# Another order for the beginning of a convolution and attention kernel: biases by products, one norm moved to the keys, last stores on ScalarE's queue

## The chip, the cores and the metric

The kernel runs on one core of a Trainium2 chip. A core has TensorE (PE: matrix products into PSUM), VectorE (DVE), ScalarE (ACT), GpSimd (POOL) and SyncE (SP); each works through its own queue of instructions in order, and they wait for each other by semaphores. DMA transfers are issued from the queues of SP, ACT and POOL. The metric is the device time of one execution in microseconds (us), the median of several runs.

## The reference

For a batch x of shape (4, 384, 48, 48), all in float32:

```
inv   = bn_gamma * rsqrt(bn_var + 1e-5)
local = depthwise_conv7x7(x, conv_w) * inv + (bn_beta - bn_mean * inv)
xn    = layernorm(x over channels) * ln_gamma + ln_beta
q, k, v = split(xn @ qkv_w.T + qkv_b)         # 8 heads of 48
q     = q + layernorm(local over channels)    # same ln_gamma, ln_beta
a     = softmax(q @ k.T * 48**-0.5) @ v       # over all 2304 positions
out   = x + a @ proj_w.T + proj_b
```

## The kernel before

**Tiles.** Channels lie on partitions, in CC = 3 blocks of 128. An image of 2304 positions is cut into NG = 6 groups of G = 384 (eight rows of 48). With four images there are NT = 24 groups, numbered t = 6b + g. All weights stay on the chip.

**Stages.** The beginning loads weights, folds the norm's gain into the projection weights, and makes keys, values and queries of image 0 for all six groups (`from_x`, steps of two products each, taken by `next(making)`). Attention of one group runs over 12 slots with two halves each (`attend`): four pairs of heads, three slots for each. `score` makes products of keys and queries (line 730), ScalarE takes their exponential (L738), and `weigh` multiplies by the values (L751). Between two images lies the stage of keys: for each of its six groups values, keys and queries of the new image and the output products of the old one. Behind the last attention (line 978 on) the output products of the last image's six groups remain: the tail.

**Convolution.** Its 49 taps for three channel blocks are 147 VectorE instructions for each group (L245 for the first tap, L249 for the others), which run behind TensorE's work all through the kernel. For the first group ten taps of channel block 0 are done on TensorE with diagonal matrices (`first_products`, L268). A generator (`conv_ops`) yields after each instruction; `convolve_first(n)` takes n in the beginning, `convolve(point)` takes as many as `plan` has given to a point of the schedule. `plan` starts from what the beginning has done, adds estimates of VectorE's spare time at each point (`spare`, `spare_at_keys`), and sets a rate so that group t's convolution is complete before slot 6 of group t - 1 (slot 8 for t = 1), where its layernorm begins.

**Norms.** Two kinds of layernorm go along: of the convolution's result (one for each group), and of x for the coming image (`norm_x` in the slots, `norms_x` at the keys). Each sums over channels twice. In the beginning and for t = 0 the sums are products with a constant matrix (L376, L381); later they go over DRAM (`out`, L418 and L419, two trips for each norm). VectorE adds, centres (L391, L436) and scales (L460, L610); ScalarE squares (L354, L359) and takes the root. `query_end` (L619) adds the normed convolution to the queries. X_LATER = 3: three of an image's x-norms lie in the attention slots of the image before (its groups 3 to 5), three at the image's own keys.

**Biases.** The layernorm's offset beta reaches keys, values and queries as a bias. `shift_rows` multiplies beta by the weights, which gives one row of 384 numbers; `rows_out` copies it out of PSUM (L561), stores it to DRAM on ScalarE's queue (L566) and loads it back as a column on POOL's (L104); `key_bias` and `query_bias` add it. ScalarE folds the gain into the weights in `scale_values` and `scale_rows`.

**Order.** The order on TensorE, VectorE and ScalarE is that of the program's text. The queue of SP is ordered by the compiler of the kernel, by its own estimates of when things are ready. SP issues nearly all loads and stores. A tile taken again from a pool waits until its former use is over: residuals (`xr`) and fetched attention results (`af`) have two buffers each. `finish` (L706) adds bias and residual, and issues the store of the result (L709). PSUM is handed out in two alternating pools (`two_banks`).

**Flag.** At the end the kernel counts reciprocals of softmax denominators that are out of a safe range (`judge`: L1018 to L1024), loads the count into registers of all engines (L1027) and jumps past a second, careful version if it is zero.

The last group's attention result is multiplied with its reciprocals within the tail:

```
        if last:
            ao = outputs[before][0]
            nc.vector.tensor_mul(ao, ao, rb)
        else:
            load_residual(before + 1)
```

Of the kernel before, what the change touches and what calls it, by code (L numbers as in the profile page):

```python
# [28 lines left out]
LAG = 2  # L29
PE_TAPS = 10  # L30
# [14 lines left out]
def unshifted_pass(  # L45
# [101 lines left out]
    nc.gpsimd.memset(eps, LN_EPS)  # L147
    nc.sync.dma_start(out=norms[:, 0:4], in_=bn)
# [78 lines left out]
    def conv_ops(t):  # L227
# [9 lines left out]
        for i, tap in enumerate(taps):  # L237
            for c in range(CC) if t or i >= PE_TAPS else range(1, CC):
                part = window(slab, acc[:, c, :], g, first, end, c, tap)
                if not part:  # L240
                    continue
                src, dst = part
                weight = cw[:, c, tap : tap + 1]
                if tap == taps[0]:
                    nc.vector.tensor_scalar(  # L245
                        dst, src, weight, shift[:, c : c + 1], ALU.mult, ALU.add
                    )
                else:
                    nc.vector.scalar_tensor_tensor(dst, src, weight, dst, ALU.mult, ALU.add)  # L249
                yield  # L250
# [28 lines left out]
    def spare(t, s, half):  # L279
# [3 lines left out]
        if b + 1 < B and g >= X_LATER:  # L283
            time -= {(3, 1): 2.3, (4, 1): 2.2, (5, 1): 2.3, (7, 0): 0.4, (8, 0): 2.6}.get(
                (s, half), 0.0
            )
# [10 lines left out]
    def spare_at_keys(g, h):  # L297
        time = 4.6 - {0: 0.6, 4: 1.2}.get(h, 0.0)
        if g < NG - X_LATER:
            time -= {0: 2.3, 2: 2.2, 4: 2.3}.get(h, 0.0)  # L300
        if 0 < g <= NG - X_LATER:
            time -= {1: 0.4, 3: 2.6}.get(h, 0.0)
# [3 lines left out]
    for t in range(NT):  # L306
        if t % NG == 0 and t:
            points += [("kv", t, g, h) for g in range(NG) for h in range(5)]
            room += [spare_at_keys(g, h) for g in range(NG) for h in range(5)]
# [233 lines left out]
    rows = [None] * CC  # L543

    def shift_rows(some):
        r = two_banks()
        for j, i in enumerate(some):
            rows[i] = r[0:1, j, :C]
            project(
                rows[i],  # L550
                lambda c: beta[:, c : c + 1],
                lambda c: staged[i][:, c, :] if i < 2 else w_v[:, c, :],
            )

    def rows_out(some):

        row = work.tile([P, C, CC], F32, tag="rb", name="row", bufs=1)
        row = row.rearrange("p c n -> p (c n)")[0:1, 0 : C * len(some)]
        row = row.rearrange("o (c n) -> o c n", n=len(some))
        for j, i in enumerate(some):  # L560
            nc.scalar.copy(row[:, :, j], rows[i])  # L561
        bias = dram.tile([C, len(some)], F32, tag=f"bias{some[0]}", name="bias", bufs=1)
        columns = const.tile(
# [971 lines left out]
```

## Time and profile before

| what | us |
|---|---|
| median of 3 runs (2885.15 to 2888.23) | 2886.48 |
| the profiled execution | 2889.06 |
| its span, first to last instruction | 2887.3 |
| TensorE busy | 2841.7 |
| VectorE busy | 2351.0 |
| ScalarE busy | 1649.4 |
| first attention product, image 0 | 146.4 |
| last attention product ends | 2828.7 |
| last VectorE instruction ends | 2881.3 |

An instruction's line reads: start, length, engine, line of the program, operation, output<-inputs, partitions and sizes, how many were merged; in brackets the engine's idle time before it and what ended that. A line of waits reads: who waited for whom, total us, times, longest. In a line of stretches each engine's busy time is followed by its number of instructions, and the last columns are the granted clock of TensorE (1.00 is full speed), the share of the DMA engines' time, and GB/s.

### The profile page before, as it was taken

The page shows a single profiled execution, that of the slowest core. Times are in us where ns is not written, and L with a number is a line of the kernel's source. Part 1 is how long each engine was busy: PE and PEld are TensorE (multiplying, and loading weights), DVE is VectorE, ACT ScalarE, POOL GpSimd, SP SyncE. Part 2 cuts the span into 40 slices and gives each one's busy share as a digit, 9 for nine tenths or more (in the row PEclk, how much of TensorE's full clock was granted, in tenths as well). Part 3 has the DMA queues.
Part 4 walks back from the last instruction along what each step waited for, and adds up shares of the span by engine and source line. Part 5 has one row for each costly group of instructions (what it writes and reads, how often), then busy time and mean ns, then how long its engine had stood idle before and what let it go on. Part 6 is the DMA issues. An engine that isn't in the chain of part 4 may idle for free.

```text
span 2887.3 us, 70195 instructions
## 1 busy us (share of the span) xinstructions
PE 2841.7 (98%) x29474; PEld 1398.5 (48%) x29474; DVE 2351.0 (81%) x4661; ACT 1649.4 (57%) x2340; POOL 21.6 (1%) x89
## 2 busy tenths in 40 slices
PE   8999999999999999999999999999999999999997
PEld 4544444444554444444455445555555544444443
DVE  7899999999888988878888888888788787787301
ACT  4366666666326666666623666666642466666661
POOL 2000000000000000000000000000000000000000
PEclk9999999999999999999999999999999999999999
DMA  6101121112221111111132112102113110100003
GB/s 114 40 4 37 43 49 35 23 38 44 71 79 33 39 35 41 31 38 24 37 94 68 27 30 51 34 23 45 38 42 89 45 30 21 41 23 15 14 20 119
DMA packets 103948, 124.37 MB, mean 43 GB/s; under 512 B 43603, under 2 KB 89284, under 8 KB 103621
## 3 DMA queue, kind: packets, MB, share of 16 engines
q1 hardware_dynamic: 102160, 119.61, 17.4%
q8 instruction: 233, 3.82, 0.6%
q14 instruction: 95, 0.77, 0.1%
q0 software_dynamic: 960, 0.07, 0.0%
q10 hardware_dynamic: 500, 0.11, 0.0%
HBM read 81.98 MB, written 27.04 MB: 38 GB/s over the span
## 4 chain that ended last, share of the span: by engine, by line
PE 89%; DVE 8%; DMA 2%; ACT 0%; issue 0%; POOL 0%; SPq 0%; ACTq 0%; DVEq 0%; POOLq 0%
PE r L730 35%; PE o L751 35%; PE r L465 9%; PE o L465 9%; DVE acc L249 6%; DVE xr L706 0%; DMA xr<-in_x_dram 0%; DMA staged<-in_qkv_wT_dram 0%; DMA columns<-bias 0%; DVE sq L365 0%; DMA taps_in<-in_conv_w_dram 0%; PE r L376 0%; DMA xn<-in_x_dram 0%; DMA w_v<-in_qkv_wT_dram 0%; DVE sq L364 0%
## 5 line engine op out<-in xcount | busy, mean ns | idle before, releaser
L738 ACT ACTIVATE pt<-r 128x768 f32<-128x768 f32 x1728 | 1400.6, 811 | 757.7 <-PE r L730 741.7
L249 DVE SCALAR_TENSOR_TENSOR acc<-slab,vec,acc 128x368 f32<-128x368 f32 (+5 forms) x3447 | 1753.9, 586 | 0.0
L751 PE MATMUL o<-pt,v 64*64 64x384 f32 x13824 | 1428.2, 482 | 0.0
L730 PE MATMUL r<-xn,k 48*64 48x384 f32 x10368 | 1073.7, 483 | 10.2 <-ACT pt L738 8.2
L751 PEld LDWEIGHTS o<-pt,v 64*64 64x64 f32 x13824 | 528.0, 132 | 592.9 <-issue 588.3
L730 PEld LDWEIGHTS r<-xn,k 48*64 48x64 f32 x10368 | 395.7, 133 | 457.9 <-issue 409.2
L730 PE MATMUL r<-qt,kt 48*64 48x384 f32 x3456 | 356.3, 482 | 0.1
L730 PEld LDWEIGHTS r<-qt,kt 48*64 48x64 f32 x3456 | 130.7, 132 | 149.2 <-issue 138.7
L649 DVE TENSOR_TENSOR ao<-o,ao 113x384 f32<-113x384 f32 x72 | 40.0, 556 | 198.8 <-PE r L730 181.6
L465 PE MATMUL o<-xn,w_qk 128*128 128x384 f32 x450 | 153.3, 486 | 0.0
L465 PE MATMUL r<-xn,w_qk 128*128 128x384 f32 x414 | 141.0, 486 | 0.0
L465 PEld LDWEIGHTS o<-xn,w_qk 128*128 128x128 f32 x450 | 85.5, 190 | 59.6
L465 PEld LDWEIGHTS r<-xn,w_qk 128*128 128x128 f32 x414 | 78.7, 190 | 54.9
L497 ACT COPY v<-o 128x384 f32<-128x384 f32 x46 | 20.0, 482 | 135.2 <-PE o L465 135.2
L465 PE MATMUL o<-w_v,xn 128*128 128x384 f32 x276 | 93.4, 487 | 0.0
L465 PE MATMUL r<-af,w_o 128*128 128x384 f32 x228 | 81.8, 508 | 5.2 <-DMA af<-held 3.1
L649 DVE TENSOR_TENSOR aot<-o,aot 113x384 f32<-113x384 f32 x24 | 13.4, 557 | 79.2 <-ACT aot L640 62.2
L364 DVE TENSOR_TENSOR sq<-sq 128x384 f32<-128x384 f32 x47 | 26.1, 555 | 55.6 <-ACT sq L359 55.5
L465 PEld LDWEIGHTS o<-w_v,xn 128*128 128x128 f32 x276 | 52.2, 190 | 37.5 <-issue 1.8
L465 PEld LDWEIGHTS r<-af,w_o 128*128 128x128 f32 x228 | 44.5, 197 | 38.5 <-DVE xr L706 4.5
L706 DVE SCALAR_TENSOR_TENSOR xr<-o,pb,xr 128x384 f32<-128x384 f32 x26 | 16.1, 618 | 53.4 <-ACT xn L516 42.4
L503 ACT ACTIVATE k<-o,qkb 128x384 f32<-128x384 f32 x48 | 25.5, 579 | 53.0 <-PE o L465 53.0
(125 smaller groups left out, 1058.7 us busy)
## 6 DMA issues: line engine op xcount, KB each, us to landing
xr<-in_x_dram SPq DMA_DIRECT2D x24, 576.0 KB
out_dram<-xr SPq DMA_DIRECT2D x72, 192.0 KB
slab<-in_x_dram SPq DMA_DIRECT2D x32, 378.0 KB
held<-ao SPq DMA_DIRECT2D x20, 576.0 KB
af<-held SPq DMA_DIRECT2D x20, 576.0 KB
xn<-in_x_dram SPq DMA_DIRECT2D x48, 216.0 KB
rb<-rden SPq DMA_DIRECT2D x48, 216.0 KB
slab<-in_x_dram SPq DMA_DIRECT2D x16, 297.0 KB
```

The costliest lines, as they stand in the source:

```text
L249: nc.vector.scalar_tensor_tensor(dst, src, weight, dst, ALU.mult, ALU.add)
L364: nc.vector.tensor_add(self.buf[:, 0, :], src[:, 0, :], src[:, 1, :])
L465: nc.tensor.matmul(dst, lhsT=weights(c), rhs=src(c), start=c == 0, stop=c == CC - 1)
L497: nc.scalar.copy(v[:, blk, :, 0:HD], r[:, :C].rearrange("p (h d) -> p h d", d=HD))
L503: nc.scalar.activation(k[:, u, :], r[:, :G], AF.Identity, bias=qkb[:, 1, u : u + 1])
L649: nc.vector.tensor_add(dst, sums[0 : 64 + HA, 1, :G], dst)
L706: nc.vector.scalar_tensor_tensor(xr[:, co, :], m, pb[:, co : co + 1], xr[:, co, :], ALU.add, ALU.add)
L730: nc.tensor.matmul(r[h, j, :G], lhsT=kk[:, blk * P + h.start : blk * P + h.stop], rhs=qq, start=True, stop=True,)
L738: nc.scalar.activation(pt, r[:, :, :G], AF.Exp, scale=SCALE)
L751: nc.tensor.matmul(sums[halves[j], i, :G], lhsT=values[t // NG, kb // NB][h, first : first + 64], rhs=pt[h, j, :], start=kb == 0, stop=kb ...
```

## The change

- **Beginning.** All six groups of image 0 now follow one order. The first group's special order of convolution steps (8 of channel block 0's taps first, then blocks 1 and 2, then the rest) is new, and so are the numbers of steps taken at each place.
- **Biases.** `rows_out` goes. `shift_rows` now writes rows to partition 0 or 64 and copies them to SBUF, in the weights' head order; `columns` turns each row into columns by products of one row with the number one. The queries' row is made within the first group.
- **Norms.** For image 1 alone, `later` is 4: four of its x-norms lie beside its keys and two in the attention slots of image 0. The estimates for `plan` follow.
- **Tail.** The stores of the last six groups are issued on ScalarE's queue. The second group's residual and attention result are requested in the last attention, later ones one group earlier in the text. The count comes ahead of the second group's products, the last multiply after the third group, and the register loads ahead of the last group's products.

```diff
+AHEAD = 8
...
+    one = const.tile([P, 1], F32, tag="one", name="one")
+    nc.gpsimd.memset(one, 1.0)
...
-        for i, tap in enumerate(taps):
-            for c in range(CC) if t or i >= PE_TAPS else range(1, CC):
...
+        order = [(tap, c) for tap in taps for c in range(CC)]
+        if t == 0:
+            mine = [(tap, 0) for tap in taps[PE_TAPS:]]
+            order = mine[:AHEAD] + [o for o in order if o[1]] + mine[AHEAD:]
+        for tap, c in order:
...
-        if b + 1 < B and g >= X_LATER:
+        if b + 1 < B and g >= later(b + 1):
...
+    def later(b):
+
+        return X_LATER + (b == 1)
+
-    def spare_at_keys(g, h):
+    def spare_at_keys(b, g, h):
         time = 4.6 - {0: 0.6, 4: 1.2}.get(h, 0.0)
-        if g < NG - X_LATER:
+        if g < later(b):
             time -= {0: 2.3, 2: 2.2, 4: 2.3}.get(h, 0.0)
-        if 0 < g <= NG - X_LATER:
+        if 0 < g <= later(b):
             time -= {1: 0.4, 3: 2.6}.get(h, 0.0)
...
-    rows = [None] * CC
+
+    row = work.tile([P, CC, P], F32, tag="rb", name="row", bufs=1)
+
+    def of_row(i):
+        return slice(0, 1) if i == 2 else slice(64, 65)
 
     def shift_rows(some):
         r = two_banks()
+        for c in range(CC):
+            for i in some:
+                nc.tensor.matmul(
+                    r[of_row(i), i % 2, :C],
+                    lhsT=beta[:, c : c + 1],
+                    rhs=staged[i][:, c, :] if i < 2 else w_v[:, c, :],
+                    start=c == 0,
+                    stop=c == CC - 1,
+                )
+        for i in some:
+            src, dst = r[of_row(i), i % 2, :C], row[of_row(i)]
+            dst = dst.rearrange("o u (h d) -> o u h d", h=2)
+            nc.scalar.copy(
+                dst[:, :, :, 0:HD], src[:, 0:288].rearrange("o (u h d) -> o u h d", h=2, d=HD)
+            )
+            nc.scalar.copy(
+                dst[:, :, :, HD:64],
+                src[:, 288:384].rearrange("o (h u r) -> o u h r", h=2, r=16),
+            )
+
+    def columns(some):
+
+        m = two_banks()[:, :, 0:CC]
         for j, i in enumerate(some):
...
+            for c in range(CC):
+                nc.tensor.matmul(
+                    m[:, j, c : c + 1],
+                    lhsT=row[of_row(i), c, :],
+                    rhs=one[of_row(i)],
+                    start=True,
+                    stop=True,
+                )
+        return m
...
-    def finish(t, co, m):
+    def finish(t, co, m, queue=nc.sync):
...
-        nc.sync.dma_start(
+        queue.dma_start(
             out=out[b, co * P : (co + 1) * P, g * G : (g + 1) * G], in_=xr[:, co, :]
         )
...
     make_diagonals()
     first_products(3)
-    convolve_first(2)
     norm = Norm(xn[0, 0])
     norm.mean_of(norm.src)
-    first_products(1)
-    shift_rows((2, 1))
-    convolve_first(4)
+    convolve_first(AHEAD)
     norm.centre()
     norm.squares()
-    columns = rows_out((1, 2))
-    convolve_first(4)
+    first_products(3)
+    shift_rows((2, 1))
+    scale_values()
+    convolve_first(12)
     norm.mean_of(norm.buf)
     norm.root()
-    shift_rows((0,))
-    first_products(6)
-    scale_values()
-    columns_q = rows_out((0,))
-    convolve_first(4)
-    norm.scale(norm.newton())
+    first_products(4)
+    m = columns((1, 2))
     for c in range(CC):
         scale_rows(1, c)
+    norm.scale(norm.newton())
+    key_bias(m)
     for g in range(NG):
 
         last = g == NG - 1
         making = from_x(0, g)
         next(making)
-        if g == 0:
-            scale_rows(0, 0)
-        convolve_first(10 if last else 4)
+        convolve_first(4)
+        norm = Norm(accs[0] if last else xn[0, g + 1])
+        norm.sum()
+        norm.mean()
         if g == 0:
             add_products()
-        norm = Norm(accs[0] if last else xn[0, g + 1])
-        norm.sum()
-        if g == 0:
-            key_bias(columns)
-        if last:
-            next(making)
-        norm.mean()
-        convolve_first(3)
+        convolve_first(5)
         norm.centre()
         norm.squares()
         next(making)
         if g == 0:
-            scale_rows(0, 1)
-            scale_rows(0, 2)
+            shift_rows((0,))
         convolve_first(3)
         norm.sum_squares()
         norm.mean()
         norm.root()
+        if g == 0:
+            for c in range(CC):
+                scale_rows(0, c)
         next(making)
         if g == 0:
-            query_bias(columns_q)
-        next(making)
-        next(making, None)
-        convolve_first(5 if last else 13)
+            m = columns((0,))
+        convolve_first(8 if last else 13)
         if last:
             local_end(0, norm.newton())
-            query_end(0)
         else:
             norm.scale(norm.newton())
+        if g == 0:
+            query_bias(m)
+        next(making)
+        next(making)
+    query_end(0)
...
-                new = X_LATER + gk if X_LATER + gk < NG else None
+                new = NG - later(b) + gk if gk < later(b) else None
...
                 else:
                     load_residual(t - g)
+                    load_residual(t - g + 1)
+                    coming_ao = fetch(t - g + 1)
...
         last = before == NT - 1
-        if last:
-            ao = outputs[before][0]
-            nc.vector.tensor_mul(ao, ao, rb)
-        else:
-            load_residual(before + 1)
+        if before == NT - NG + 1:
+            judge[0](two_banks()[:, 0, :])
...
-            finish(before, co, m)
+            finish(before, co, m, nc.scalar)
+        ao = coming_ao
+        if before + 3 < NT:
+            coming_ao = fetch(before + 2)
+        else:
+            coming_ao = outputs[NT - 1][0]
         if before + 2 < NT:
-            ao = fetch(before + 1)
+            load_residual(before + 2)
         if before == NT - NG:
             rb = divide(NT - 1)
         if before == NT - NG + 1:
-            judge[0](two_banks()[:, 0, :])
+            judge[1]()
         if before == NT - NG + 2:
-            judge[1]()
+            nc.vector.tensor_mul(outputs[NT - 1][0], outputs[NT - 1][0], rb)
+        if before == NT - 2:
+            n_outside = judge[2]()
+    return n_outside
```

## The prediction

> **What bounds the kernel now.** I read the page first, then the list of TensorE's waits, then busy time by stage, then the timelines of the stages that lose time. The profiled execution took 2889.1 us with a span of 2887.3, 2.6 above the median of 2886.5; sums are made on the span and their difference is taken off the median.
>
> ```profile
> PE 2841.7 (98%) x29474; PEld 1398.5 (48%) x29474; DVE 2351.0 (81%) x4661; ACT 1649.4 (57%) x2340; POOL 21.6 (1%) x89
> ...
> PE   8999999999999999999999999999999999999997
> PEld 4544444444554444444455445555555544444443
> DVE  7899999999888988878888888888788787787301
> ```
>
> TensorE (PE) is busy 98% and sets the pace; only its idle time and its slow stretches can be won. VectorE (DVE) averages 81%, but reads 9 in slices 3 to 10, which are the first image. TensorE's waits:
>
> ```profile
> PE o L268 <- DMA vec<-natural: 12.5, 1, 12.5
> PE r L730 <- ACT pt L738: 8.2, 5, 2.9
> PE r L381 <- DVE sq L365: 4.4, 1, 4.4
> PE r L465 <- DMA af<-held: 3.1, 1, 3.1
> ...
> PE r L465 <- DVE xr L706: 2.8, 4, 0.7
> PE r L730 <- DVE xr L706: 2.0, 3, 0.8
> PE r L465 <- DVE ao L985: 2.0, 1, 2.0
> ```
>
> The first stays: line 268 still waits for the taps. The next two lie in image 0 and the rest in the tail. By stage:
>
> ```profile
> 146.00:218.40 72.40, 67.85 (x820) 31.88 (x818) 72.37 (x143) 43.19 (x56) 0.00 (x0) 0.99 0.02 4
> 218.40:728.00 509.60, 501.46 (x6092) 231.28 (x6096) 497.97 (x997) 331.94 (x457) 0.81 (x10) 0.99 0.17 38
> 728.00:730.20 2.20, 2.20 (x29) 0.79 (x21) 0.12 (x1) 0.81 (x1) 0.00 (x0) 1.00 0.00 0
> 730.20:866.00 135.80, 135.80 (x422) 80.03 (x422) 117.77 (x229) 32.58 (x67) 0.16 (x2) 1.00 0.29 79
> ```
>
> The columns are window, length, then busy time of PE, weight loads, DVE, ACT, POOL. VectorE is full from 146 to 218; at the keys (730 to 866) it has 18 us free and TensorE none. Attention of image 0 runs from 146.4 to 730.2, 583.8 us; that of image 1 from 871.3 to 1429.8, 558.5. Of the 25 us more, some 3 to 4 are work of its own (two pairs of means, the output bias), the rest is VectorE's lateness. Idle is only part of it:
>
> ```profile
> 218.46 1.62 PE L381 MATMUL r<-sq,mean_w 128*128 128x384 f32 x2 [4.42 <-DVE sq L365]
> ...
> 222.62 1.50 PE L730 MATMUL r<-xn,k 48*64 48x384 f32 x8
> 223.91 1.07 PE L751 MATMUL o<-pt,v 64*64 64x384 f32 x8
> 224.81 0.82 PE L730 MATMUL r<-xn,k 48*64 48x384 f32 x8
> ```
>
> After an idle of 4.4 us the rows need 1.28 from start to start in place of 0.65, at a granted clock of 0.66 in that stretch, and lose 2.9 more. The idle of 2.92 at 313 loses 1.7 more, that of 1.96 at 508 also 1.7. So image 0 loses 7.3 (t=0), 4.6 (t=1), 1.4 (t=2), 1.7+1.96+1.7 (t=3) and about 1 in small waits: 19.7.
>
> **Image 0: taps.** I worked the plan's arithmetic through with both sets of constants. The beginning now issues 8+12+5x25+20=165 steps, before 14+5x23+21=150, so 15 steps leave image 0. A tap costs 0.516 (60 in 30.95). Moving one x-norm out of t=3 also takes from VectorE there, up to the point where t=3's own norm is centred, about 6.8 (sum with transpose and reduction 2.3, few, transpose, centre 2.2, second sum 2.3). At the centring that TensorE waits for, the steps done since attention began change by -7, -15, -20, -13 at t=0 to 3 (the plan spreads them anew).
> - t=0: VectorE 7x0.516=3.6 earlier, idle 4.4 becomes 0.8, no slow stretch.
> - t=1: TensorE's delay was 7.9+2.9=10.8; VectorE is 15x0.516=7.7 earlier and loses 0.6 less to an idle of its own at 244: delay 2.4, of which some 1.6 was spent before, idle 0.8.
> - t=2: delay before 10.8+1.7+0.5+1.4=14.4; 20 steps and the 0.6 take 10.9: 3.5.
> - t=3: before 14.4+1.7+2.0=18.1 (the 1.7, at 490, waits for the x-norm that leaves); now less 6.7 (13 steps), 6.8 and 0.6: 4.0.
> - t=4, t=5: no waits before, and 11 to 15 steps fewer now.
> About 4 of 19.7 remain, in gaps under 1.5: **-15.5**. Bounds: -9, if one gap stays over 2 us and the second norm point of t=0, whose margin falls from 2.4 to about 0, adds; -18, if nothing remains.
>
> A rule against the row: the Trainium skill, "TensorE: Matmul & The Clock Gate", section "Why this matters for your kernels", allows idle gaps up to about 3 us before the rate drops. Here 1.96 and 2.92 were followed by a drop; 1.43, 1.69 and the tail's 1.98 were not. By the rule only the first gap's 2.9 were clock and t=1 and t=3 would hold nothing to win from it (-12); I go by the rows.
>
> **Keys of image 1.** Here a fourth norm is added, its two trips over DRAM (two writes and two reads on SP's queue, ahead of later stores and loads there) too; against its 9 us of VectorE stand 14 taps fewer (158 to 144), 7.2. It fits in 18 us: 0. The lead shrinks: each norm was scaled over a group ahead of its use, now in the group just before. The rows: scaling ends at 772.55 and 796.54, the next groups start at 776.68 and 799.90, so 4.1 and 3.4 us are left. Value 0; with the cover gone each missing us is a wait of TensorE, four times over.
>
> **Beginning.** TensorE is busy nearly without a gap from 12.5 to 146, so work moved within it counts where it opens one. Out go POOL's eight column loads and ScalarE's two bias stores; VectorE's wait for columns (1.2 idle at 40) goes, but it was cover, 0. Step by step, TensorE at 18.25 after the first mean: three products to 20.2; six row products of 0.645 to 24.1; the second mean to 26.0. ScalarE can copy the rows only at 24.1: four copies of about 0.35 (the 384-wide row took 0.45) to 25.5, w_v's scaling 1.6 to 27.1, root 1.7 to 28.8; it is the late one now. VectorE: newton 1.85 and scaling 1.37, to 32.1. TensorE has done four products and the columns by 30 and waits 2.1. The nearest row for a column product is the output bias (18 records of 128x1, some 0.12 each), so 0.7 for three of them and 1.4 for six, the six ahead of a wait. First value product: 32.1 against 30.77, +1.4. The query's row products, once in front of it, come later, +1.9, their columns +0.7. VectorE in groups 0 and 1 gets two more taps each where it had no idle (18.3 of 19.7, 18.7 of 19.3): +0.4 net; in groups 2 to 4 it idles 1.6 to 3.3 waiting for means, which covers 1.0. The gap of 2.1 lies between 1.96, which lost 1.7, and the 1.98 that lost nothing: +0.9 as the mean. Eight taps of block 0 start when its weights are there (12.0 against 14.3), while VectorE waited: 0. Last group: 20 taps and the norm are 17 of 19 us, 0. Sum **+5** (2.5 to 7).
>
> **Tail.** Last attention ends at 2828.7, VectorE's last instruction at 2881.3, the span at 2887.3.
>
> ```profile
> 2853.62 4.21 PE L465 MATMUL r<-af,w_o 128*128 128x384 f32 x6 [3.08 <-DMA af<-held]
> 2858.54 4.21 PE L465 MATMUL r<-af,w_o 128*128 128x384 f32 x6 [0.71 <-DVE xr L706]
> 2862.54 2.29 PE L465 MATMUL o<-af,w_o 128*128 128x384 f32 x6
> ```
>
> and of SP's own waits in the tail (total, times, longest):
>
> ```profile
> SPq L709 <- DVE xr L706: 26.1, 13, 4.6
> ```
>
> SP's queue stands 26.1 us before stores whose sums aren't ready, and the next fetch stands behind them; so the row of 3.08 and the slow 4.21s (normal 2.2). The same skill, "Trainium Kernel Development and Optimization", section "Key Constraints", says that issuing from several engines saves only issue time. By that rule alone the move is worth 0 (bytes and engines unchanged). The row shows head-of-line waiting, which it doesn't count; I follow the row. A group is 6.9 us (2828.61 to 2835.50, with the 0.7 wait inside). Six are 41.3. The count now stands ahead of the second group: its reciprocal waits for the denominators (SP at 2834.1, landing 1.8 later) and for the third sum, so the count is at 2837.4 where the group would start at 2835.5: 2.0 against 1.0. The last multiply (1.98 wait) is done groups ahead. The early loads of group 19 change nothing: the tail issues three fetches and four residuals already. A residual needs its buffer's store landed (0.65+0.4+2), then 4.2 to 5: 7.6 to 8.3 after the group's end, and is wanted at 9.0: hidden by 1 us; without that cover each is 1 to 3. The flag's register loads (0.5 each) run in idle. VectorE's end 2872.6; from there 6.0 before, now 5.7, since ScalarE's last store is followed by a jump as SP's was (2.7; ScalarE's took 4.5 under load: +2 at worst). **End 2878.3, -9; with a chance of slow clock after 1.9 us, -8.6** (-3 to -10).
>
> Sum: 5-15.5-8.6=-19.1, so 2867.4.
>
> **Rivals.**
> 1. Half of image 0's delay comes back at the second norm points and at query ends (margin 0 there): -8 in place of -15.5, 2875. For it: VectorE stays near full to 520. Against: no wait longer than 0.5 there now.
> 2. The tail stays led by loads, as its residuals have only 1 us of cover: -3, 2873.
> 3. The beginning costs 2.5 and image 0 gives 18, tail 9.5: 2861.5. For it: every bound on the good side is a row's.
> 4. Slower: the four norms at image 1's keys come late. If scaling ends 7 us later than now (twice the 3.4 left), each of four groups waits 3.5 and loses up to 2.9 to the clock, 25.6: 2893. VectorE there waits up to 1.6 for one trip over DRAM; it takes a trip of over twice that.
> That the taps don't move is no rival: the plan fixes the counts.
>
> **Numbers.** As summed 0.60 (alone 2860 to 2873), first rival 0.16, second 0.08, third 0.12, fourth 0.04. Range 2857 to 2877 leaves out the slower one and the edges. 0.2% (5.8 us) is what a measurement can tell: same is 2880.7 to 2892.3, the first rival's far end, 0.03; slower 0.04; faster 0.93.
>
> **What would show it.** The wait of line 381 under 1.5, no clock below 0.95 in 216 to 226; image 0's attention 568 us, starting near 151; a new wait near 30 for scaled xn; no wait for held in the tail, the count's at 1.5 to 2; tail 50 from last attention to the end. Wrong if the gap in the beginning reaches 4, or waits for xn's scaling stand at 750 to 850.

## Result and profile after

The changed kernel takes **2870.4 us** (median of six runs, 2870.26 to 2870.88) against 2887.4 for the kernel before on the same chip: a ratio of 0.994, 95% interval 0.9927 to 0.9952. The forecast was 2867.4, range 2857 to 2877. The span fell from 2887.3 to 2868.5, by 18.8, where the prediction's sum was 19.1; the median moved by 17.0.

In the changed kernel's lines the projection's products are L475 (before L465), the means L386 and L391 (L376, L381), scores L754 and values L775 (L730, L751), ScalarE's exponential L762, a convolution step L255 (L249), the tail's addition L730 (L706) and its store L733 (L709). First the busy times from its page, then the list of TensorE's waits (total, times, longest):

```profile
PE 2835.0 (99%) x29492; PEld 1383.8 (48%) x29492; DVE 2353.2 (82%) x4661; ACT 1648.1 (57%) x2341; POOL 17.3 (1%) x82
```

```profile
PE o L274 <- ACT pt L263: 12.2, 1, 12.2
PE r L475 <- DVE xr L730: 5.2, 5, 1.8
PE o L475 <- DVE xn L470: 2.3, 1, 2.3
PE r L754 <- DVE xr L730: 2.0, 3, 0.8
PE o L1046 <- DVE outside L1044: 1.7, 1, 1.7
PE r L386 <- DVE sq L375: 1.5, 2, 1.3
PE r L754 <- ACT pt L762: 1.3, 3, 0.6
```

Gone from the top of that list are the 4.4 of the second mean, 6.9 of the 8.2 for exponentials, the 3.1 for `held` and the 2.0 for `ao`. New are 2.3 for a scaled xn and 1.3 for a mean in the beginning, and in the tail 1.7 for the count and more for additions (5.2, before 2.8).

The stretches of the first image, then of image 1's keys (window, length, busy time of PE, weight loads, VectorE, ScalarE, POOL, then the granted clock):

```profile
151.72:220.00 68.28, 68.09 (x811) 32.64 (x814) 66.84 (x132) 41.88 (x55) 0.00 (x0) 0.98 0.09 16
220.00:719.75 499.75, 498.61 (x6133) 246.93 (x6125) 484.40 (x970) 331.59 (x454) 0.82 (x10) 1.00 0.16 37
721.00:860.00 139.00, 139.00 (x437) 81.46 (x435) 122.92 (x240) 34.23 (x70) 0.00 (x0) 1.00 0.29 79
```

TensorE is idle for 1.3 us of image 0's attention, where the two rows of before leave 12.7 (4.55 and 8.14), and never at the keys (139.00 of 139.00).

Cut into stages the two profiles differ as follows. An image's attention is taken from its first product to the start of its last row of value products, here and in every kernel below.

| stage | before | after | change |
|---|---|---|---|
| start to TensorE's first product | 12.46 | 12.20 | -0.3 |
| beginning, to the first attention product | 133.9 | 139.5 | +5.6 |
| attention of image 0 | 581.7 | 565.9 | -15.8 |
| images 1 to 3 with their keys | 2098.5 | 2098.4 | 0.0 |
| tail | 60.7 | 52.4 | -8.3 |

The first row is the arrival of the first loads. It lay between 10.9 and 12.5 in the fourteen profiles, with nothing in the text that would explain it, so whole spans carry 1.6 us of chance, and the experiments are compared by stages.

### The profile page after: what moved, and what is told of

It is laid out like the page before. It is cut to its first block, busy times and chain, and to the rows that moved or that the text cites. A ratio compares the mean times of both kernels' runs of the same rounds, so it can differ in the third digit from the quotient of the medians.

```text
span 2868.5 us, 70244 instructions
## 1 busy us (share of the span) xinstructions
PE 2835.0 (99%) x29492; PEld 1383.8 (48%) x29492; DVE 2353.2 (82%) x4661; ACT 1648.1 (57%) x2341; POOL 17.3 (1%) x82
## 4 chain that ended last, share of the span: by engine, by line
PE 96%; DVE 2%; DMA 1%; ACT 0%; issue 0%; POOL 0%; SPq 0%; ACTq 0%; DVEq 0%
PE r L754 39%; PE o L775 39%; PE r L475 9%; PE o L475 9%; DVE acc L255 1%; DVE xr L730 0%; DMA out_dram<-xr 0%; PE o L274 0%; DMA taps_in<-in_conv_w_dram 0%; DMA rb<-rden 0%; PE r L563 0%; DVE xn L470 0%; DVE xn L401 0%; ACT pt L762 0%; PE o L386 0%
## 5 line engine op out<-in xcount | busy, mean ns | idle before, releaser
L762 ACT ACTIVATE pt<-r 128x768 f32<-128x768 f32 x1728 | 1398.7, 810 | 757.5 <-PE r L754 741.3
L255 DVE SCALAR_TENSOR_TENSOR acc<-slab,vec,acc 128x368 f32<-128x368 f32 (+7 forms) x3447 | 1757.2, 586 | 5.2 <-DMA xn<-in_x_dram 4.1
L775 PE MATMUL o<-pt,v 64*64 64x384 f32 x13824 | 1423.9, 482 | 0.0
L754 PE MATMUL r<-xn,k 48*64 48x384 f32 x10368 | 1070.2, 482 | 3.2 <-DVE xr L730 2.0
L775 PEld LDWEIGHTS o<-pt,v 64*64 64x64 f32 x13824 | 520.5, 132 | 598.3 <-issue 575.2
L754 PEld LDWEIGHTS r<-xn,k 48*64 48x64 f32 x10368 | 391.6, 132 | 452.8 <-issue 394.2
L754 PE MATMUL r<-qt,kt 48*64 48x384 f32 x3456 | 354.5, 482 | 0.1
L754 PEld LDWEIGHTS r<-qt,kt 48*64 48x64 f32 x3456 | 126.8, 132 | 153.1 <-issue 142.8
L475 PE MATMUL r<-xn,w_qk 128*128 128x384 f32 x444 | 151.3, 487 | 0.0
L475 PE MATMUL o<-xn,w_qk 128*128 128x384 f32 x420 | 143.1, 486 | 0.0
L475 PEld LDWEIGHTS r<-xn,w_qk 128*128 128x128 f32 x444 | 84.4, 190 | 58.5
L475 PEld LDWEIGHTS o<-xn,w_qk 128*128 128x128 f32 x420 | 79.9, 190 | 55.5
L475 PE MATMUL o<-w_v,xn 128*128 128x384 f32 x270 | 93.3, 496 | 2.7 <-DVE xn L470 2.3
L475 PE MATMUL r<-af,w_o 128*128 128x384 f32 x234 | 79.9, 489 | 4.5 <-DVE xr L730 4.5
L475 PEld LDWEIGHTS o<-w_v,xn 128*128 128x128 f32 x270 | 51.6, 193 | 40.8 <-issue 5.9
L475 PEld LDWEIGHTS r<-af,w_o 128*128 128x128 f32 x234 | 44.1, 190 | 36.7 <-DVE xr L730 7.0
L730 DVE SCALAR_TENSOR_TENSOR xr<-o,pb,xr 128x384 f32<-128x384 f32 x25 | 15.5, 618 | 51.5 <-ACT xn L526 41.6
L475 PE MATMUL r<-w_v,xn 128*128 128x384 f32 x162 | 56.2, 486 | 0.0
```

The lines of the kernel that those rows point to most:

```text
L475: nc.tensor.matmul(dst, lhsT=weights(c), rhs=src(c), start=c == 0, stop=c == CC - 1)
L730: nc.vector.scalar_tensor_tensor(xr[:, co, :], m, pb[:, co : co + 1], xr[:, co, :], ALU.add, ALU.add)
L754: nc.tensor.matmul(r[h, j, :G], lhsT=kk[:, blk * P + h.start : blk * P + h.stop], rhs=qq, start=True, stop=True,)
L762: nc.scalar.activation(pt, r[:, :, :G], AF.Exp, scale=SCALE)
L775: nc.tensor.matmul(sums[halves[j], i, :G], lhsT=values[t // NG, kb // NB][h, first : first + 64], rhs=pt[h, j, :], start=kb == 0, stop=kb ...
```

## Experiments

Each kernel below is the changed kernel with one edit, unless more is said. This table has the stages of the profiled executions and the medians; "before" on the same chips was 2886.9 to 2887.8.

| kernel | beginning | image 0 | images 1-3 | tail | median | ratio to before |
|---|---|---|---|---|---|---|
| after | 139.5 | 565.9 | 2098.4 | 52.4 | 2870.4 | 0.994 |
| after_again | 138.9 | 565.9 | 2098.4 | 51.4 | 2869.1 | 0.9936 |
| norms_3 | 139.7 | 571.4 | 2098.5 | 51.0 | 2874.7 | 0.9954 |
| taps_150 | 141.0 | 571.2 | 2098.4 | 52.0 | 2876.2 | 0.9958 |
| taps_150_norms_3 | 141.9 | 576.7 | 2098.5 | 52.4 | 2881.7 | 0.9977 |
| tail_before | 140.1 | 565.8 | 2098.4 | 58.9 | 2875.8 | 0.9958 |
| tail_sp | 139.5 | 565.7 | 2098.4 | 60.0 | 2877.4 | 0.9967 |
| rows_serial | 140.2 | 566.0 | 2098.4 | 51.9 | 2869.6 | 0.9938 |
| rows_in_gap | 137.3 | 565.6 | 2098.5 | 51.6 | 2864.9 | 0.9922 |
| dummy_in_gap | 137.6 | 566.1 | 2097.3 | 51.4 | 2865.7 | 0.9925 |
| flip | 136.8 | 566.0 | 2097.3 | 52.3 | 2866.4 | 0.9927 |
| best | 135.4 | 564.6 | 2098.4 | 50.9 | 2862.8 | 0.9915 |
| best_flip | 136.3 | 564.7 | 2097.3 | 49.7 | 2863.5 | 0.9917 |

The row after_again is the changed kernel unaltered, beside the last three:

> The changed kernel itself, unaltered, beside the next three on one chip: 2870.4 within 1 us. Its first product started at 12.2 us where the other profiles have 10.9 to 11.7; if that is the kernel's own, it is 12.2 here too, if it is chance, somewhere from 10.9 to 12.5.

It took 2869.1 (2867.95 to 2870.13), 1.3 under the six runs of the first table. So 1.3 us between kernels that were not measured together means nothing.

### Image 0: steps, norm, and both

In all fourteen profiles the length of image 0's attention, up to the end of its last product, is 564.2 to 565.1 us plus two things: TensorE's idle time, and half of the time that it worked at half clock (the granted clock is 0.50 or 1.00, see the last section).

| kernel | idle | lost at half clock |
|---|---|---|
| before | 12.7 | 6.4 |
| after | 1.3 | 1.7 |
| norms_3 | 5.3 | 3.4 |
| taps_150 | 6.8 | 2.3 |
| taps_150_norms_3 | 11.0 | 2.7 |

The first edit:

```diff
     def later(b):
-        return X_LATER + (b == 1)
+        return X_LATER
```

> The changed kernel with one thing undone: three of image 1's x-norms beside its keys, as before, so t=3 of image 0 has its x-norm again; the 15 taps stay in the beginning. Account of the prediction: at t=3's centring VectorE has 6.8 us more to do, less one for two taps fewer, and no slack there (busy 99% from 150 to 450), so TensorE waits some 5 to 6 and loses 1.7 at a reduced clock where one gap passes 2 us: 4 to 8 us slower than the changed kernel (2870.4), about 2876. Rival, the norm was covered in image 0 as it is at the keys, and all of the gain came from the 15 taps: within 1 us.

Image 0 is 5.5 longer, inside the expected 4 to 8; the median is 4.3 higher. TensorE's rows at the norm's place:

```profile
408.27 0.88 PE L754 MATMUL r<-xn,k 48*64 48x384 f32 x8 [3.08 <-ACT pt L762]
408.96 1.46 PE L775 MATMUL o<-pt,v 64*64 64x384 f32 x8
410.19 1.51 PE L754 MATMUL r<-xn,k 48*64 48x384 f32 x8
...
505.44 0.88 PE L754 MATMUL r<-xn,k 48*64 48x384 f32 x8 [1.95 <-ACT pt L762]
506.14 0.83 PE L775 MATMUL o<-pt,v 64*64 64x384 f32 x8
```

One x-norm more on VectorE in image 0 brings back an idle of 3.08 with slow products behind it (1.46 and 1.51 in place of 0.83), and one of 1.95 without. In the changed kernel the same places wait 0.48 and 0.59. The rival, that this norm was covered in image 0 as it is at the keys, would have left 565.9; it falls.

The second kernel takes the number of steps done in the beginning back from 165 to 150:

```diff
-    convolve_first(12)
+    convolve_first(6)
...
-        convolve_first(4)
+        convolve_first(10 if last else 4)
...
-        convolve_first(5)
+        convolve_first(3)
...
-        convolve_first(8 if last else 13)
+        convolve_first(5 if last else 13)
```

> The changed kernel with the numbers of the kernel before in the beginning: 150 convolution steps in place of 165, the rest as changed. Account of the prediction: the wait of the first mean of t=0 returns with 4.4 us of idle and 2.9 of reduced clock, t=1's with 2.9 and 1.7, and the 1.3 us that the beginning's fifth group now waits goes: 7 to 10 us slower than the changed kernel, about 2878.5. Rival, VectorE makes the 15 taps up in its idle time at t=4 and t=5 and TensorE waits no more than now: within 2 us.

Image 0 grew by 5.3, the beginning by 1.4; the median by 5.8, under the expected 7 to 10. The beginning was expected to shrink by 1.3: the wait in its fifth group did fall from 1.32 to 0.44, but one of 2.17 came in its last group. The waits in image 0 are not those of the kernel before:

```profile
136.87 0.88 PE L386 MATMUL o<-sq,mean_w 128*128 128x384 f32 x2 [2.17 <-DVE sq L375]
...
221.93 0.88 PE L391 MATMUL r<-sq,mean_w 128*128 128x384 f32 x2 [1.56 <-DVE sq L375]
...
318.59 1.56 PE L754 MATMUL r<-xn,k 48*64 48x384 f32 x8 [4.62 <-ACT pt L762]
```

At t = 0 only 1.56 of 4.42 came back, and no slow stretch behind it; at t = 1 it is 4.62 where 2.92 stood before. Most likely TensorE, no longer held up at t = 0, met VectorE's lateness a group later.

Both edits together:

> Both undone together in the changed kernel: 150 steps and three norms. If the two are one account of VectorE's lateness, which is only spent once, image 0's attention takes about 584 us again (568.0 as changed), 13 to 16 us more than the changed kernel, about 2885; about the sum of the two single ones. If they are independent of each other and of the order of the beginning, it is that sum; if the new order of the beginning had helped image 0 by itself, it is less than 12.

Image 0 takes 576.7: 10.8 more than in the changed kernel, the sum of 5.3 and 5.5, so no interplay of the two is seen. 13 to 16 was expected, and less than 12 only if the new order of the beginning helps image 0 by itself. With steps and norm both as before, image 0 is still 5.0 shorter than in the kernel before (581.7). By the table above it has 1.7 less idle time and loses 3.7 less to the clock. VectorE's rows where the attention of image 0 begins, in the kernel before and in this one:

```profile
147.21 31.03 DVE L249 SCALAR_TENSOR_TENSOR acc<-slab,vec,acc 128x368 f32<-128x368 f32 x60
```

```profile
148.95 1.68 DVE L643 SCALAR_TENSOR_TENSOR xn<-acc,vec,xn 128x384 f32<-128x384 f32 x3
150.54 31.03 DVE L255 SCALAR_TENSOR_TENSOR acc<-slab,vec,acc 128x368 f32<-128x368 f32 x60
```

The same 60 steps take the same 31.03. But before, VectorE began them 0.85 *after* TensorE's first attention product (146.36), and here it begins 3.02 *before* it (153.56). TensorE's longer beginning is a head start of 3.9 for VectorE, of which VectorE loses 0.93 again to a wait for ScalarE at 182.5. What is left agrees with the wait at t = 0, which is 2.86 shorter than before (1.56 for 4.42) and has no slow stretch behind it (3.0 before): 5.8 us. At t = 1 some 2.7 of that are lost again (a wait of 4.62 for 2.92, and 2.7 of slow clock for 1.7), and t = 2 gives 1.0. At t = 3 the waits are as before (1.80 and 1.95 for 1.69 and 1.96), but the slow stretch of 1.7 behind the last is missing, which follows from where the gap fell (last section). So the head start is the likely cause of some 3 of the 5.0, not of all; it was not tried by itself. In the changed kernel it is smaller: VectorE starts its steps at 150.02, 1.70 ahead of TensorE (151.72), 2.55 more than before.

### The tail: whole, and the queue alone

The edit of tail_before puts the whole text of the tail back: stores on SP's queue, one fetch and one residual at a time, count after the second group, last multiply and register loads in their old places.

```diff
-                    load_residual(t - g + 1)
-                    coming_ao = fetch(t - g + 1)
...
-            finish(before, co, m, nc.scalar)
+            finish(before, co, m)
-        ao = coming_ao
...
         if before + 2 < NT:
-            load_residual(before + 2)
+            ao = fetch(before + 1)
```

> The changed kernel with the whole tail of the kernel before: stores on SP's queue, count after the second group, last multiply and register loads at the end. By the account: 50.4 us from the last attention product to the end become 58.6, so 8 us slower, about 2878.5. Rival, the tail is bound by its bytes and the gain seen there belongs to an earlier end of the loads: within 2 us.

The tail takes 58.9, 6.5 more than in one profile of the changed kernel and 7.5 more than in the other, and the waits of 3.15 for `held` and 1.98 for `ao` are back. The median grew by 5.4, where 8 was expected.

The other kernel changes one argument, the queue of the last 18 stores:

```diff
-            finish(before, co, m, nc.scalar)
+            finish(before, co, m)
```

> The changed kernel with the stores of the last six groups on SP's queue again, and nothing else: the count, the multiply, the early loads and the register loads stay as changed. Head-of-line waiting: fetches and residuals stand behind stores whose sums are not ready, a wait for a fetched result and slow products return, 3 to 7 us slower than the changed kernel (2870.4). Rival, the queue's choice saves only the time of issue (18 stores of 0.35 us, covered by TensorE): within 1 us.

The tail takes 60.0, where the kernel before has 60.7 and tail_before 58.9: next to nothing of its gain is left. The median is 2877.4. What waits, however, isn't a fetched result. SP's queue, and then TensorE in the same stretch:

```profile
2822.58 1.00 SPq L733 DMA_DIRECT2D out_dram<-xr  x2
2824.10 0.33 SPq L724 DMA_DIRECT2D af<-held  x1
2824.75 0.33 SPq L733 DMA_DIRECT2D out_dram<-xr  x1
2825.14 0.42 SPq L690 DMA_DIRECT2D rd<-den  x1
```

```profile
2830.09 0.24 PE L1046 MATMUL o<-outside,ones_col 128*1 128x24 f32 x2 [6.02 <-DVE outside L1044]
2830.26 4.21 PE L475 MATMUL r<-af,w_o 128*128 128x384 f32 x6
2835.17 4.03 PE L475 MATMUL r<-af,w_o 128*128 128x384 f32 x6 [0.71 <-DVE xr L730]
```

The fetch of the last denominators (`rd<-den`) stands behind three stores of group 18, each of which waits for its addition, and behind a fetch of 576 KB. It leaves at 2825.14, 8.1 after the last attention product, and takes 3.83 to land. The reciprocals come late, and the count, which the change moved ahead of the second group, holds TensorE for 6.02; then twelve records of products run at half speed (4.21 and 4.03 for a normal 2.20), another 3.8 us. In the changed kernel the stores are gone from that queue. The fetch leaves 5.5 after the last attention product, ahead of the 576 KB, and has landed within 2.1. SP's row, and TensorE's:

```profile
2823.67 0.54 SPq L690 DMA_DIRECT2D rd<-den  x1
```

```profile
2826.81 0.21 PE L1046 MATMUL o<-outside,ones_col 128*1 128x24 f32 x2 [1.66 <-DVE outside L1044]
2826.95 2.20 PE L475 MATMUL r<-af,w_o 128*128 128x384 f32 x6
...
2844.56 2.20 PE L475 MATMUL r<-af,w_o 128*128 128x384 f32 x6 [1.84 <-DVE xr L730]
...
2851.89 2.20 PE L475 MATMUL r<-af,w_o 128*128 128x384 f32 x6 [1.26 <-DVE xr L730]
```

By the rule that issuing from several engines saves only issue time (the Trainium skill, "Trainium Kernel Development and Optimization", section "Key Constraints"), tail_sp would have stood within 1 us of the changed kernel. Its tail is 7.6 to 8.6 longer, and its median 7.1 to 8.3. The edit changes nothing but the queue of the 18 stores. Of the 4.4 by which the count waits longer, some 2.6 are the later issue and 1.8 the slower landing; what slows the landing, the stores or the large fetch just ahead, was not tried by itself.

### The beginning: the row products, the gap, the clock

The prediction gave the six row products 3.9 us, one after another. The changed kernel's trace shows 2.04, since records of `w_v` (row on partition 0) and of `staged` (partition 64) run side by side. Does that need the two to alternate in the text?

```diff
-        for c in range(CC):
-            for i in some:
+        for i in some:
+            for c in range(CC):
```

> The changed kernel with the loops of the first row products swapped: three for the values' row, then three for the keys', in place of alternating. In the changed kernel six took 2.0 us where 3.9 was predicted. If alternating products that write partitions 0 and 64 overlap in TensorE, the six take 3.9 here, ScalarE's copies and so the first value product come 1.9 us later: 1.5 to 2.5 slower. Rival, one-column weights are quick as such: the same time within 0.5 us and still 2.0 for six.

The median is 2869.6, like the changed kernel's. TensorE's rows:

```profile
19.72 1.13 PE L563 MATMUL r<-w_v,vec 128*1 128x384 f32 x3
20.37 0.48 PE L563 MATMUL r<-staged,vec 128*1 128x384 f32 x1
20.69 0.49 PE L563 MATMUL r<-w_v,vec 128*1 128x384 f32 x1
...
21.34 1.13 PE L563 MATMUL r<-staged,vec 128*1 128x384 f32 x3
22.40 2.20 PE L475 MATMUL o<-sq,mean_w 128*128 128x384 f32 x6
```

Though all of `w_v`'s products stand first in the queue, `staged` starts two records later and runs beside the rest; the six take 2.7, as they did in after_again with the alternating text (2.75). So the alternation isn't needed for the overlap. Nor are one-column products quick as such, as the rival had it: in the kernel before, whose rows all go to partition 0, the same six take 3.96, one after another:

```profile
18.95 2.10 PE L465 MATMUL r<-w_v,vec 128*1 128x384 f32 x6
20.89 2.10 PE L465 MATMUL r<-staged,vec 128*1 128x384 f32 x6
```

The next product there starts at 22.91. The different partition is thus what the overlap goes with.

In the gap of 2.3 us ahead of the first value product TensorE could do the query's row products, which stand 10 us later:

```diff
         scale_rows(1, c)
+    shift_rows((0,))
     norm.scale(norm.newton())
...
         next(making)
-        if g == 0:
-            shift_rows((0,))
```

> The changed kernel with the queries' row products moved from within the first group into TensorE's gap of 2.3 us ahead of the first value product. They take 2.0 there instead of in the group (-1.9), and if the reduced clock behind that gap (twelve records in 5.8 us in place of 4.0) comes from the gap, it goes too (-1.8): 3 to 4 us faster, about 2866.7. Rival, the reduced clock there is left over from the start: only 1.5 to 2.2 faster.

```profile
27.72 2.10 PE L563 MATMUL o<-staged,vec 128*1 128x384 f32 x6
29.75 4.14 PE L475 MATMUL r<-w_v,xn 128*128 128x384 f32 x12
...
39.73 0.88 PE L386 MATMUL o<-sq,mean_w 128*128 128x384 f32 x2 [1.33 <-DVE sq L375]
```

The gap is gone, the twelve value records take 4.14 in place of 5.80, and 2.0 us of products left the place where they cost something. Of those 3.7 a new wait took back 1.33: the squares for the second group's norm are the next thing late, once TensorE arrives earlier. The beginning is 2.3 shorter; the median is 4.2 under after_again. In the profiles the first product is 1.1 earlier, which no edit explains.

Three products that nobody reads fill the gap without removing work elsewhere:

```diff
         scale_rows(1, c)
+    unread = two_banks()[0:1, 0, :C]
+    project(unread, lambda c: beta[:, c : c + 1], lambda c: w_v[:, c, :])
```

> The changed kernel with three extra products in the gap ahead of the first value product; they multiply one column of weights with the values' weights and nobody reads what they give. No work is taken off the path, so only the clock can change. If the gap lowers it: 1.8 us faster. If not: same within 0.4 us, or slower if they reach past the gap.

The beginning is 2.0 shorter than in the changed kernel and the value records take 4.14, 1.7 less: so the clock's loss goes when the gap is filled. The median is 2865.7. But the edit also takes one PSUM bank pair and so turns which of the two pools every later product gets, and images 1 to 3 are 1.1 shorter, where nothing was expected. So that was made alone, with no instruction changed:

```diff
     key_bias(m)
+    next(either)
     for g in range(NG):
```

> The changed kernel with one turn of the alternation of the two PSUM pools skipped ahead of the first group; no instruction is added or taken away. The kernel with extra products in the gap was 4.6 us faster where the clock explains 2.0; it also turned the alternation by one. If that is the rest, the three waits of attention's first products for the last output sums at the image changes (2.0 us together) go: 1.5 to 2.5 faster than the changed kernel. If the rest is chance at the start: within 0.5.

Images 1 to 3 take 2097.3 again, as in the other two kernels with the turned order, against 2098.4 to 2098.5 in the ten without. The wait of 2.0 for additions at the keys' output products (L754 for L730, three times) is no longer in the list. The median is 2.7 under after_again; 1.1 of that is the turn. Most of the rest lies in the beginning, which is 2.1 shorter in the profile, although flip has the gap that dummy_in_gap fills:

```profile
29.19 4.11 PE L475 MATMUL r<-w_v,xn 128*128 128x384 f32 x12 [1.81 <-DVE xn L470]
```

```profile
29.82 5.53 PE L475 MATMUL o<-w_v,xn 128*128 128x384 f32 x12 [1.81 <-DVE xn L470]
```

The first is flip, the second after_again: the same products behind the same gap of 1.81, without and with a slow clock. So a gain of 1.4 us can come there without the gap being filled, and dummy_in_gap alone doesn't prove what its gain came from; what decides is in the last section.

### What the waits point to

The kernel called best has the row products in the gap, two convolution steps moved from the first group (where the 1.33 opened) to the last, a third buffer for residuals, and the count one group later:

```diff
+        xr = work.tile([P, CC, G], F32, tag="xr", name=f"xr{t}", bufs=3)
...
+    shift_rows((0,))
...
+        convolve_first(5 if g else 3)
...
+        convolve_first(10 if last else 13)
...
+        if before == NT - NG + 2:
             judge[0](two_banks()[:, 0, :])
```

> The queries' row products in the gap (2864.9 alone, with a new wait of 1.3 for VectorE in the first group), two taps moved from the first group to the last so that this wait goes (-1.0), a third residual buffer, so that the tail's waits of 1.8 and 1.3 shrink to 0.7 (-1.7), and the count one group later, where its sum is long ready (-1.7): 2860 to 2862. If the residual waits are set by the loads and not by the buffers, 1.7 less gain.

It takes **2862.8** (ratio 0.9915 to before, 0.9898 to 0.9931), 6.3 under after_again; a touch over the expected 2860 to 2862. Its waits:

```profile
PE r L475 <- DVE xr L730: 2.8, 4, 0.7
...
PE o L1045 <- DVE outside L1043: 0.8, 1, 0.8
```

The tail's 1.84 and 1.26 are back at 0.7 each and the count waits 0.8; a wait of 1.05 stands where the count was. The beginning still waits 1.37 at 117.4. Adding flip's line:

> The kernel before this one with the alternation of the PSUM pools turned by one as well: another 1.5 to 2.5 faster, about 2859, if the waits at the image changes are what it takes away; else the same as that one.

2863.5: no gain over best that these runs can tell. In the profiles its images 1 to 3 are 1.1 shorter, as in flip, and its tail 1.2; its beginning is 0.9 longer. That the turn adds to best is not shown.

## Why the prediction was right

**Image 0** (forecast -15.5: 568 us from about 151). It begins at 151.72 and ends at 719.75: 568.0. The wait of the second mean is gone, with a clock of 1.00 there. The prediction's 19.7 of lost time comes out as 19.1 (12.7 idle and 6.4 clock). Of its about 4 that were to remain in waits, 1.3 did; against that, a slow stretch nobody had counted lost 1.7 (last section). Moving the norm is worth 5.5 and the steps 5.3, both shown by their undoing, and that is the mechanism that was forecast. But they make 10.8 and not 15.5: that the sum was met is in part luck. **The step that failed** took it that VectorE and TensorE would begin image 0 as far apart as before, though the same prediction made TensorE's beginning 5 us longer. VectorE begins 2.55 earlier against TensorE than before, so the +5 held half of a gain that wasn't booked, and that the kernel before lost 1.7 to the clock at t = 3 hung on where its gap of 1.96 fell (last section). (Attention of image 1 begins at 869.65 in the kernel before, not at 871.3, so image 0 took 23.6 more and not 25; no sum rests on it.)

**Keys** (forecast 0, with 18 us of VectorE free). TensorE worked all 139.00 of 139; images 1 to 3 are equal to 0.1. The fourth rival, four late norms at the keys, fell.

**Beginning** (forecast +5; +5.6 measured). Terms: six row products 2.0 us, not 3.9, since they overlap, so the first value product comes 18.2 after TensorE's first product, where it was 18.3 before: -0.1 for the +1.4 forecast. The gap is 2.3 (forecast 2.1). Slow clock +1.7 (forecast +0.9, the mean of nothing and 1.7). Query rows 2.0 (1.9), columns 0.75 (0.7). Two waits were not forecast:

```profile
122.05 0.89 PE L386 MATMUL r<-sq,mean_w 128*128 128x384 f32 x2 [1.32 <-DVE sq L375]
```

and 0.30 at 37.12 for ScalarE's value copy. The 1.32 is where the prediction let idle time of VectorE in groups 2 to 4 cover 1.0. There 13 steps took 7.71 in the changed kernel, where the same group's 13 took 5.68 before:

```profile
101.21 7.71 DVE L255 SCALAR_TENSOR_TENSOR acc<-slab,vec,acc 128x360 f32<-128x360 f32 x13
```

```profile
97.41 5.68 DVE L249 SCALAR_TENSOR_TENSOR acc<-slab,vec,acc 128x360 f32<-128x360 f32 x13
```

Only 0.6 of these 2.0 is width: the 13 lengths sum to 7.28 and 6.66. The rest goes with the order. The change puts 8 and later 31 steps of channel block 0 in a row, and each of them starts 0.035 after the end of the one before; where steps go from block to block, in both kernels, the next starts about 0.085 before that end. That is 0.12 for each of some 38 steps, 4.6 us of VectorE's time by this estimate, and the prediction's mean price of a step missed it. All changed kernels have this order, so that it causes the 1.32 is not shown. The beginning's sum was right through errors on both sides.

**Tail** (forecast -8.6; -8.3 between these two profiles). The count waits 1.66 (forecast 2.0), no wait for `held` or `ao`, no slow clock. "Hidden by 1 us" failed for two residuals: the waits of 1.84 and 1.26 are 1.7 more than the usual 0.7 twice, with SP waiting up to 5.3 for the store that frees a buffer; the third buffer in best removed them. From VectorE's last instruction (2863.47) to the end it is 5.0, forecast 5.7. From last attention product to the end: 50.3, forecast 50. That the gain hangs on the queue was the argument, and tail_sp showed it, with the count and not a fetched result as the one that waits.

**The clock.** The prediction gave the beginning's gap half of a slow stretch (+0.9), since 1.96 had one and 1.98 had none. Both readings are right, but the length of the gap isn't what decides (last section).

**The rivals.** Half of image 0's delay didn't come back (first). The tail wasn't led by loads, though the second rival's mechanism, late residuals, took 1.7 of the 5.6 that it would have cost. The good sides of all bounds (third) weren't reached together: the beginning alone took 5.6.

## What to carry to other kernels

When an edit makes the leading engine's stretch longer, the engines that run behind it get a head start there; count how far apart the two begin the next stage before adding up. A store that waits for a late result belongs in a queue in which nothing urgent stands behind it: here one argument of the call was worth 7 us or more. And when a wait is filled, look at once at what is late next, for in rows_in_gap it took back a third of the gain.

## What was not expected of the hardware

**Gaps and the clock.** The same twelve value products in the beginning, normally 4.03 to 4.14, stood behind gaps of different length:

| gap ahead | kernels | the twelve records took |
|---|---|---|
| 2.32 | after, norms_3, taps_150_norms_3, tail_before, tail_sp | 5.80 in each |
| 1.81 | after_again, taps_150, rows_serial | 5.53, 5.78, 5.80 |
| 1.81 | flip | 4.11 |
| 0.61 | best_flip | 4.14 |
| none | before; rows_in_gap, dummy_in_gap, best | 4.03; 4.14 |

In the attention, gaps up to 1.80 and the two of 1.95 in norms_3 and taps_150_norms_3 were followed by no drop, those of 1.96 (before), 2.92, 3.08, 4.42 and 4.62 by one. By the Trainium skill's figure of about 3 us for a gap without loss ("TensorE: Matmul & The Clock Gate", section "Why this matters for your kernels"), the drop behind 1.96 would not have come.

What decides can be read from the times at which the granted clock changes. In each profile they lie on one grid of 3.41 us: 17.00, 30.65, 34.06, 180.84, 184.25 in the changed kernel. Where the grid lies differs from profile to profile. Two windows of it in after_again, then two in flip, with the same gap of 1.81 (28.01 to 29.82, and 27.38 to 29.19):

```profile
25.87:29.29 3.42, 2.14 (x16) 1.37 (x14) 2.71 (x4) 3.39 (x13) 0.00 (x0) 1.00 1.10 198
29.29:32.70 3.41, 2.88 (x5) 1.70 (x6) 3.38 (x9) 0.34 (x2) 0.00 (x0) 0.50 1.08 196
```

```profile
24.81:28.22 3.41, 2.57 (x18) 1.67 (x16) 2.27 (x4) 3.38 (x12) 0.00 (x0) 1.00 1.08 194
28.22:31.63 3.41, 2.44 (x8) 1.55 (x9) 3.39 (x8) 0.78 (x4) 0.00 (x0) 1.00 1.08 203
```

In after_again 1.28 of the gap and 1.01 of the tiny `columns` products ahead of it lie in one window, together 2.29, and the next window runs at half clock. In flip an edge cuts the gap: 0.85 of it and 1.0 of the tiny products in the first window, 0.96 in the second, and no drop. Count in each window the time in which TensorE was idle or on products of one column. In the fourteen profiles, from 14 us on, 40 windows at full clock had 1.83 or more of it and a window at half clock behind them; among them are all with 1.92 or more. None with 1.80 or less did, and two more, with 1.85 and 1.91, did not. So here it was not one long gap that counted but more than about 1.85 of 3.41 us in one window, and a gap of 1.95 got by where an edge cut it (1.10 and 1.35 in the fuller window), while one of 1.96 did not (1.93). One window at half clock costs 1.7 us.

**Tiny products and the clock.** The output bias is 18 records of 128x1. TensorE counts as busy throughout, yet in the changed kernel slow products follow:

```profile
178.27 2.17 PE L475 MATMUL r<-vbp,w_o 128*128 128x1 f32 x18
...
181.28 1.52 PE L775 MATMUL o<-pt,v 64*64 64x384 f32 x8
```

```profile
177.42:180.84 3.42, 3.42 (x38) 2.55 (x34) 2.27 (x7) 1.34 (x3) 0.00 (x0) 1.00 0.00 0
180.84:184.25 3.41, 3.41 (x28) 1.39 (x24) 3.41 (x7) 0.87 (x2) 0.00 (x0) 0.50 0.00 1
```

A slow window follows the output bias in nine of the fourteen profiles (after, after_again, norms_3, tail_before, tail_sp, rows_serial, rows_in_gap, dummy_in_gap, flip) and none in before, both taps_150 kernels and both best ones. No edit was aimed at it. The grid separates them: in the nine 1.90 to 2.17 of the 2.17 us lie in one window, in the other five an edge cuts them and the larger part is 1.27 to 1.86. So this 1.7 us is likely to be chance of the execution and not a property of the kernel. Two runs of one kernel can differ in it: the profiled run of rows_in_gap has a mean clock of 0.999, which the one slow window makes, and its other three runs have 1.000, too high for a whole slow window. Against it stands that the six runs of the changed kernel lie within 0.6 us.

**Rows on two partitions overlap.** Products with one column of weights that write partition 0 and partition 64 run side by side, also when one set stands wholly ahead of the other in the queue: six took 2.0 to 2.7 us where nothing held them up (up to 3.1 in dummy_in_gap and best, where the load of `staged` came late), against 3.96 on one partition.
